# Cross attention on one core: the attention's cast and low part issued a slot later, and GpSimd's low probabilities put ahead of its normalization

## The chip, the cores and the metric

The kernel runs on one core of a Trainium2 chip. A core has a matrix engine (TensorE, in the profile PE, with its weight loads as PEld), a vector engine (VectorE, DVE), an engine for functions of one value (ScalarE, ACT), a general one (GpSimd, POOL) and one that here only issues transfers (SyncE, SP). Each works through its own queue of instructions in order, and semaphores tell one engine that another is done. The metric is the device time of the whole program in microseconds, as the median of several runs. Lower is better.

## The reference

For each of 32 sequences, 512 queries of 640 channels attend to 77 keys of a context in 20 heads of 32 channels. The context has 77 rows, so the object, others and image parts of the reference are empty, and what is left is this:

```python
q = _heads(hidden_states @ to_q_w)
s = jnp.einsum('bhqd,bhkd->bhqk', q, _heads(ehs_txt @ to_k_w)) / np.sqrt(HD)
p = jax.nn.softmax(s, axis=-1)
h_txt = jnp.einsum('bhqk,bhkd->bhqd', p, _heads(ehs_txt @ to_v_w))
out = _merge(h_txt) @ to_out_w + to_out_b
out = out + residual
```

Inputs and outputs are float32: x is (32, 512, 640), the context (32, 77, 1024), the output (32, 512, 640).

## The kernel before

**Two parts for each number.** [...] So each factor is held as a high part, its cast, and a low part, the original minus the cast. A product is three matmuls (`PAIRS`): high by high, high by low, low by high. The usual maker of such a pair is `split` (lines 102 to 104): ScalarE casts, then VectorE subtracts, so that the subtraction waits for the cast.

**The order is written out by hand.** After `manual_schedule` each engine runs its instructions in the order in which the program issues them. A first stage, some 272 us long, projects keys and values of all sequences and stores them in DRAM. Then comes the main loop: `slot(n)` for n = 0 to 159, where n = 5 b + j stands for batch (sequence) b and chunk j of four heads. `end()` finishes what hangs over.

**One slot.** In each slot several chunks are in work at different stages:

- `scores(n, t)` for t = 0 to 3 multiplies queries by keys on TensorE (L453) into the tile `sc` (three buffers), and VectorE takes the negated maximum of each head (L461, `nm`). `exps(n, t)` on ScalarE makes the exponentials into `pn` and their sums (L471).
- `queries(n + 1, ...)` makes the next chunk's queries (L434, tile `pq`), and `split_q(n + 1)` splits them (`qt`).
- For the chunk before, `sums(n - 1)` takes the reciprocals of the sums on VectorE (L481, `rs`), `normalize(n - 1, rs)` multiplies `pn` by them on GpSimd (L486), and `transpose_p(n - 1)` transposes them on VectorE into `z` (L493) and sends them to DRAM (L500).
- Two slots later `load_p` brings the transposed probabilities back (`raw`, L509 and L510). In slot n the chunk `taken` = n - 3 (`LAG`) is split: `cast_p` casts the first 128 rows of each half (L517, ScalarE), `rest_p` casts the last 64 (L523, ScalarE) and makes the low part of the first 128 on VectorE (L524), and `last_p` makes the low part of the last 64 on GpSimd (L531). All of it goes into the tile `pp`, of which there is one buffer.
- `values(taken)` multiplies these probabilities by the values: six matmuls into `pa` (L545), of which the last two read what `last_p` wrote. `sum_a` copies half of `pa` on ScalarE (L556) and adds it to the other on VectorE (L558, twice) into `aw`, of which there is one buffer. `split_a` splits this attention into `at` (L103 on ScalarE, L104 on VectorE; eight buffers).
- `piece(...)` is the output projection of an earlier batch: matmuls of `at` by the output weights into `po` (L584; two banks). `finish` adds each closed bank to the residual on VectorE (L613), which frees the bank. The first pieces of a batch read the `at` of chunk n - 4 in the slots j = 2 and j = 3.
- Beside these, `split_x` casts parts of the next input on ScalarE (L262) and subtracts on GpSimd (L263) in the slots j = 2 (two) and j = 3 (three), `transpose_x` transposes it on VectorE (L255), and `add_bias` adds the bias to the residual on GpSimd (L577).

**The order around the change.** At a slot's end ScalarE issues `exps(n, 3)` and then the cast of `at`, VectorE the two sums of `aw` and then the low part of `at`. The next slot begins with `cast_p` on ScalarE and the first maximum on VectorE, then `rest_p` on both, `sums` on VectorE. On GpSimd, `normalize` goes ahead of `last_p` in slots in which an output projection runs (`has_out`); in the first few slots it is the other way round. `take(m)`, used by the last slot and by `end()`, calls `values`, `sum_a` and `split_a` at once.

## Time and profile before

| | |
|---|---|
| median of 3 runs | 2055.46 us (2054.43 to 2056.07) |
| the profiled execution, its own time | 2056.36 us |
| its span, first to last instruction | 2054.2 us |
| mean granted TensorE clock | 0.991 |
| from the first `scores` to the last chunk's | 272 to 1999 us |
| a batch of five slots, in the steady part | 54.30 us |
| DMA, share of 16 engines in 330 to 1990 us | 0.84 |

How such a profile is read: the page lists for each engine its busy time with the share of the span and the number of instructions. Its groups show a line of the code, the engine, the operation, the tiles it writes and reads, the shape and the count; then the busy time in us, the mean time of one in ns, and the idle time of the engine just before them, with what ended most of it. The table of waits has who waited for whom, in total us, times and the longest. A timeline lists instructions of one engine or all in order: start in us, how long, engine, line, operation; like ones in a row are merged (x4), and idle time ahead of one stands in square brackets with what ended it. That releaser is inferred from semaphores: of several it names the last.

An instruction on VectorE or ScalarE can start some 0.1 us before the one ahead of it is shown to end.

### The profile page before, as it was taken

What the parts mean: (1) busy time and instruction counts of PE and PEld (TensorE: products, weight loads), DVE (VectorE), ACT (ScalarE), POOL (GpSimd) and SP (SyncE); (2) the same over time, 40 slices, a digit from 0 to 9 for tenths busy, and PEclk for the clock granted to TensorE, in tenths of its full rate; (3) what the DMA queues carried; (4) which work ended last, traced back from release to release, by engine and by line L of the source; (5) the groups of instructions that cost most, each with busy time, mean ns of one, the idle gap of its engine ahead of it and who ended that gap; (6) DMA issues with size and microseconds to landing.
All of it is one profiled execution on the core that took longest, in us unless ns stands there. A gap on an engine that the chain in (4) does not pass through costs nothing.

```text
span 2054.2 us, 36186 instructions
## 1 busy us (share of the span) xinstructions
PE 1952.5 (95%) x10332; PEld 1694.3 (82%) x10332; DVE 1464.6 (71%) x2334; ACT 1547.1 (75%) x6210; POOL 1002.7 (49%) x648
## 2 busy tenths in 40 slices
PE   9999997999999999999999999999999999999997
PEld 7787886888888888888888888888888888888886
DVE  4444447777777777777777777777777777777774
ACT  3232248888888888888888888888888888888882
POOL 1000125555555555555555555555555555555543
PEclk9999998999999999999999999999999999999998
DMA  9878778888888888888888888888888888888874
GB/s 185 200 182 232 183 199 210 228 215 218 217 213 211 223 212 212 212 210 218 211 221 214 218 212 220 218 213 214 219 215 209 223 215 213 212 213 214 214 191 137
DMA packets 568277, 431.26 MB, mean 210 GB/s; under 512 B 195344, under 2 KB 477072, under 8 KB 568080
## 3 DMA queue, kind: packets, MB, share of 16 engines
q1 hardware_dynamic: 564848, 417.65, 80.6%
q0 software_dynamic: 3136, 11.14, 1.5%
q8 instruction: 84, 1.38, 0.3%
q14 instruction: 113, 0.93, 0.1%
q10 hardware_dynamic: 96, 0.16, 0.0%
HBM read 247.17 MB, written 181.64 MB: 209 GB/s over the span
## 4 chain that ended last, share of the span: by engine, by line
PE 36%; DVE 15%; issue 15%; DMA 12%; POOL 10%; ACT 6%; SPq 5%; POOLq 0%; ACTq 0%; DVEq 0%
PE po L584 11%; PE pq L434 9%; PE pa L545 6%; POOL pn L486 6%; PE sc L453 5%; DMA pd<-z 5%; DVE pp L524 4%; POOL pp L531 4%; DMA raw<-pd 3%; DVE aw L558 3%; SPq L500 2%; DVE z L493 2%; PE pk L191 2%; DVE nm L461 2%; ACT at L103 2%
## 5 line engine op out<-in xcount | busy, mean ns | idle before, releaser
L471 ACT ACTIVATE pn<-sc,nm 128x77 f32<-128x77 f32 x2560 | 800.3, 332 | 48.6 <-DVE nm L461 33.7
L486 POOL TENSOR_TENSOR pn<-pn,rs 128x1232 f32<-128x1232 f32 x160 | 364.0, 2275 | 736.0 <-DVE rs L481 442.5
L584 PE MATMUL po<-wo_s,at 128*128 128x320 f32 x3840 | 629.3, 312 | 11.1 <-DVE xr L613 3.4
L434 PE MATMUL pq<-xt,wq_s 128*128 128x512 f32 x2400 | 606.0, 393 | 0.0
L584 PEld LDWEIGHTS po<-wo_s,at 128*128 128x128 f32 x3840 | 577.1, 189 | 28.1 <-DVE xr L613 22.7
L471 ACT ACTIVATION_READ_ACCUMULATOR pn<-sc,nm 128x1 f32 x2560 | 541.3, 211 | 0.0
L434 PEld LDWEIGHTS pq<-xt,wq_s 128*128 128x128 f32 x2400 | 437.0, 188 | 75.2
L453 PE MATMUL sc<-kb,qt 128*128 128x308 f32 x1920 | 378.5, 306 | 11.2 <-ACT pn L471 5.6
L461 DVE TENSOR_REDUCE nm<-sc 128x4 f32<-128x308 f32 x640 | 291.2, 456 | 132.3 <-PE sc L453 132.2
L453 PEld LDWEIGHTS sc<-kb,qt 128*128 128x128 f32 x1920 | 325.6, 189 | 55.2 <-ACT pn L471 10.9
L545 PE MATMUL pa<-pp,vb 128*128 128x512 f32 x960 | 291.0, 415 | 66.0 <-POOL pp L531 55.8
L493 DVE STREAM_TRANSPOSE z<-pn 128x1280 f32<-128x1280 f32 x160 | 241.8, 1511 | 116.1 <-POOL pn L486 94.6
L556 ACT COPY aw<-pa 64x1024 f32<-64x1024 f32 x160 | 162.0, 1012 | 165.0 <-PE pa L545 164.9
L545 PEld LDWEIGHTS pa<-pp,vb 128*128 128x128 f32 x960 | 164.4, 190 | 146.0 <-POOL pp L531 127.8
L104 DVE TENSOR_TENSOR at<-aw,at 128x512 fp32r<-128x512 f32 x160 | 138.7, 867 | 135.3 <-ACT at L103 135.3
L531 POOL TENSOR_TENSOR pp<-raw,pp 64x512 fp32r<-64x512 f32 x160 | 208.7, 1305 | 51.5 <-ACT pp L523 39.5
L558 DVE TENSOR_TENSOR aw<-pa,aw 64x512 f32<-64x512 f32 x320 | 216.0, 675 | 23.8 <-ACT aw L556 21.6
L263 POOL TENSOR_TENSOR xt<-xs,xt 128x512 fp32r<-128x512 f32 x160 | 203.3, 1296 | 34.8 <-ACT xt L262 34.7
L577 POOL TENSOR_TENSOR xr<-xr,bias 128x640 f32<-128x640 f32 x128 | 200.6, 1569 | 9.7
L524 DVE TENSOR_TENSOR pp<-raw,pp 128x1024 fp32r<-128x1024 f32 x160 | 194.3, 1215 | 6.5 <-ACT pp L517 6.5
L517 ACT CAST pp<-raw 128x1024 fp32r<-128x1024 f32 x160 | 168.7, 1055 | 3.7 <-DMA raw<-pd 3.7
L103 ACT CAST at<-aw 128x512 fp32r<-128x512 f32 x160 | 99.8, 624 | 71.8 <-DVE aw L558 71.5
(42 smaller groups left out, 1402.6 us busy)
## 6 DMA issues: line engine op xcount, KB each, us to landing
pd<-z SPq DMA_DIRECT2D x640, 160.0 KB, 3.3
raw<-pd SPq DMA_DIRECT2D x160, 512.0 KB, 4.0
xs<-in_x_dram SPq DMA_DIRECT2D x128, 320.0 KB, 5.8
xr<-in_x_dram SPq DMA_DIRECT2D x128, 320.0 KB, 3.6
out_dram<-xr SPq DMA_DIRECT2D x127, 320.0 KB, 3.6
raw<-pd SPq DMA_DIRECT2D x160, 128.0 KB, 4.2
v_dram<-vs SPq DMA_DIRECT2D x80, 192.0 KB, 3.9
k_dram<-ks POOLq DMA_DIRECT2D x20, 512.0 KB, 3.4
```

The source lines that it names most:

```text
L263: low.tensor_tensor(parts[1], src, parts[0].bitcast(F32), ALU.subtract)
L434: nc.tensor.matmul(pqs[n], wq_s[:, k, a, j * P : (j + 1) * P], xts[b, k][:, c, :], start=(k == 0 and m == 0), stop=(k == NC_ - 1 and m == 2),)
L453: nc.tensor.matmul(sc[:, :KCOLS], qt[:, a, t * P : (t + 1) * P], kb[:, j - GROUPS[g][0], c], start=(m == 0), stop=(m == 2),)
L461: nc.vector.tensor_reduce(nm, sc[:, :KCOLS].rearrange("p (h k) -> p h k", k=NKEY), AX.X, ALU.max, negate=True)
L471: nc.scalar.activation(pnb[n % 2][:, at, :NKEY], sc[:, i * NKEY : (i + 1) * NKEY], AF.Exp, bias=nm[:, i : i + 1], accum_out=sms[n][:, at : ...
L486: nc.gpsimd.tensor_tensor(pf, pf, rs.unsqueeze(2).to_broadcast([P, NQ * HPC, NKEY]), ALU.mult)
L493: nc.vector.transpose(z.rearrange("p b t j -> p t b j"), pn.rearrange("p (t h) k -> p t (h k)", t=NQ).rearrange("p t (b i) -> p t b i", i=Q),)
L524: nc.vector.tensor_tensor(pp[:, 2:4, :], raw[:, 0:2, :], pp[:, 0:2, :].bitcast(F32), ALU.subtract)
L531: nc.gpsimd.tensor_tensor(pp[64:, 4, :], raw[:64, 2, :], pp[:64, 4, :].bitcast(F32), ALU.subtract)
L545: nc.tensor.matmul(pas[n][:, p, :], vb[:, p, t, :], pp[:, c, :], start=(c == p), stop=(t == 1),)
L558: nc.vector.tensor_tensor(aw[64 * p : 64 * p + 64, 0], pa[:64, p], aw[:64, p], ALU.add)
L584: nc.tensor.matmul(pos[b, t, h][:, :HALF], ats[b * NC_ + j][:, a, t * P : (t + 1) * P], wos[0][:, j, c, h * HALF : (h + 1) * HALF], start= ...
```

## The change

`split_a` becomes two functions, the cast and the low part. Both are no longer called at the end of the slot that made `aw`, but in the next one: the cast on ScalarE behind `cast_p` and ahead of `rest_p`'s cast, the subtraction on VectorE behind `rest_p`'s and the reciprocals. On GpSimd `last_p` now goes ahead of `normalize` in every slot. `take` calls both halves one after the other, as before. The instructions and their number stay the same.

```diff
-    def split_a(n):
+    def high_a(n):
         if n >= N - NC_ + 1:
             at = xpool[0].tile([P, 2, S], FPR, tag="xt", name="at", bufs=7)
         else:
             at = late[0].tile([P, 2, S], FPR, tag="at", name="at", bufs=8)
-        aw = aws.pop(n)
-        split(at[:, 0, :], at[:, 1, :], aw[:, 0])
+        nc.scalar.copy(at[:, 0, :], aws[n][:, 0])
         ats[n] = at
+
+    def low_a(n):
+        at = ats[n]
+        nc.vector.tensor_tensor(
+            at[:, 1, :], aws.pop(n)[:, 0], at[:, 0, :].bitcast(F32), ALU.subtract
+        )
...
     def take(m):
         values(m)
         sum_a(m)
-        split_a(m)
+        high_a(m)
+        low_a(m)
...
         if taken is not None:
             cast_p(taken)
+        if n - 1 in takes:
+            high_a(takes[n - 1])
         s = scores(n, 0)
         if taken is not None:
             rest_p(taken)
         rs = sums(n - 1) if n else None
-        if taken is not None and not has_out:
+        if taken is not None:
             last_p(taken)
         if n:
             normalize(n - 1, rs)
-        if taken is not None and has_out:
-            last_p(taken)
+        if n - 1 in takes:
+            low_a(takes[n - 1])
         exps(n, 0, *s)
...
         exps(n, 3, *s)
-        if taken is not None:
-            split_a(taken)
```

## The prediction

> **What bounds the kernel now.** I read the page first, then the table of waits, then the timelines of single engines through one batch (1087.74 to 1142.03 us of the profiled execution). A "slot" is one turn of `slot(n)`; I date it from the first matmul of `scores(n, 0)`. Slots repeat exactly by j = n % 5, and a batch of five takes 54.30 us: 10.69, 10.66, 11.07, 11.61 and 10.26 for j = 0 to 4.

> ```profile
> PE 1952.5 (95%) x10332; PEld 1694.3 (82%) x10332; DVE 1464.6 (71%) x2334; ACT 1547.1 (75%) x6210; POOL 1002.7 (49%) x648
> L104 DVE TENSOR_TENSOR at<-aw,at 128x512 fp32r<-128x512 f32 x160 | 138.7, 867 | 135.3 <-ACT at L103 135.3
> ```

> TensorE is busy 95%, so the question is where the rest goes. The table of waits (who waits for whom: us in total, times, longest) says it:

> ```profile
> DVE at L104 <- ACT at L103: 135.3, 160, 1.0
> PEld pa L545 <- POOL pp L531: 127.8, 153, 3.4
> PE pa L545 <- POOL pp L531: 55.8, 82, 2.9
> PEld po L584 <- DVE xr L613: 22.7, 62, 3.6
> ```

> The matmuls of `values` wait for the last low probabilities (L531), and some of `piece` for an output bank that L613 empties. VectorE's 135.3 us before the low part of `at` are idle time in order of program. The timelines of TensorE, GpSimd and VectorE through the slot j = 3 that begins at 1120.16 (start us, us, instruction):

> ```profile
> 1125.78 1.09 PE L545 MATMUL pa<-pp,vb 128*128 128x512 f32 x4
> 1127.86 0.73 PE L545 MATMUL pa<-pp,vb 128*128 128x512 f32 x2 [0.98 <-DMA raw<-pd]
> ...
> 1129.03 2.90 PE L584 MATMUL po<-wo_s,at 128*128 128x320 f32 x18
> ```
> ```profile
> 1124.18 2.27 POOL L486 TENSOR_TENSOR pn<-pn,rs 128x1232 f32<-128x1232 f32 x1 [2.68 <-DVE rs L481]
> 1126.54 1.27 POOL L531 TENSOR_TENSOR pp<-raw,pp 64x512 fp32r<-64x512 f32 x1
> ...
> 1129.40 3.79 POOL L263 TENSOR_TENSOR xt<-xs,xt 128x512 fp32r<-128x512 f32 x3
> ```
> ```profile
> 1122.66 1.22 DVE L524 TENSOR_TENSOR pp<-raw,pp 128x1024 fp32r<-128x1024 f32 x1
> 1123.79 0.25 DVE L481 RECIPROCAL rs<-sm 128x16 f32<-128x16 f32 x1
> ...
> 1126.49 1.51 DVE L493 STREAM_TRANSPOSE z<-pn 128x1280 f32<-128x1280 f32 x1 [0.92 <-POOL pn L486]
> 1127.93 0.65 DVE L104 TENSOR_TENSOR qt<-pq,qt 128x512 fp32r<-128x512 f32 x1
> 1128.50 0.87 DVE L613 TENSOR_TENSOR xr<-po,xr 128x320 f32<-128x320 f32 x2
> ...
> 1132.11 1.63 DVE L104 TENSOR_TENSOR at<-aw,at 128x512 fp32r<-128x512 f32 x1 [1.01 <-ACT at L103]
> ```

> Two chains are to be seen. First, rs, normalization, L531, last two `pa`: the fifth `pa` starts 2.08 after the first where four steps of 0.23 make 0.92, so TensorE loses 1.16, and 0.11 at the sixth. Second, normalization, z, qt, the first xr (ends 1128.97), `po`: 18 matmuls start at 1129.03, which is 0.29 late. Read alike, the stall at `pa` is 0.27, 0.62, 0.98, 1.27 and 0.20 for j = 0 to 4, together 3.34; at `po` it is 0.37 (j = 0) and 0.29 (j = 3). Without all of it a batch would take 50.30, some 10.06 a slot.

> **The change, part by part.** Nothing is added or removed: the same casts, subtractions and products run. Three things move. I count from E, the end of `exps(n-1, 3)` on ScalarE; in the trace it lies at -0.29 to 0.87 after the slot's beginning.

> *The cast of `at` behind the probabilities'.* Now ScalarE runs at, L517, L523 one behind the other (starts 0.53 and 0.96 apart: 1121.00, 1121.51, 1122.46), and waits up to 1.07 for aw before it. Afterwards L517 starts at E and ends at E+1.05, the cast of `at` runs E+0.96 to 1.57, L523 E+1.49 to 2.10. The sum is the same; what goes is the wait for aw, which the long L517 covers, and where aw comes later than E+0.92 the cast waits for it again.

> *Its low part behind rs on VectorE.* L524 no longer stands behind it: E+1.12 to 2.34, rs to E+2.50. The low part (0.69) could then start at E+2.42; behind it in VectorE's queue is the maximum of `scores(n, 1)`, and for that waits `exps(n, 1)`.

> *GpSimd: L531 before normalization.* L523 ends E+2.10, and GpSimd starts some 0.15 after what it waits for (rs ends 1124.04, L486 starts 1124.18): E+2.25, 1.28 long, so it ends about E+3.55. TensorE's fifth `pa` wants it at 6.5 (j = 3) or 7.4 of an unstalled slot, 1.9 later even for E = 1.12: the whole 3.34 at `pa` is off TensorE's path. Normalization would follow at E+3.6; in the slot shown it started at E+3.15, in the five slots at E+3.85 in the mean.

> *What the low part meets.* At E+2.42 to 3.55 GpSimd is in L531, then in L486. A VectorE subtraction with both inputs in SBUF does not run beside GpSimd here: the `at` row above took 1.63 instead of 0.69 and ended at 1133.74, 0.55 behind the GpSimd `xt` that ended at 1133.19; this is so in all 30 such meetings of the steady part, and that is the 867 ns mean of the page. The reverse too: L531 beside L524 in the early slots took 1.74 (ended 1.13 behind L524). What happens between two GpSimd instructions back to back shows once (VectorE, then GpSimd):

> ```profile
> 274.44 0.83 DVE L104 TENSOR_TENSOR vs<-vs 128x416 fp32r<-128x416 f32 x1 [1.15 <-ACT vs L103]
> ```
> ```profile
> 273.53 2.89 POOL L263 TENSOR_TENSOR xt<-xs,xt 128x512 fp32r<-128x512 f32 x2 [3.61 <-ACT xt L262]
> ```

> VectorE's 0.59 became 0.83, and the GpSimd pair took 2.89, not 2.55: the waiting subtraction went between the two, and the second ended 1.15 behind it. So I take: low part ends E+3.55+0.55 = 4.10; normalization ends 2.28-0.14 later, E+6.24; the maximum runs E+4.02 to 4.45 and `exps(n, 1)` starts at E+4.5, where L517-to-exps spacing alone would give E+3.3. The bounds of this unseen price: no meeting at all (low part 0.69, normalization ends E+5.9), or VectorE served only behind both (E+6.46).

> [...]

> **Slot by slot.** Later steps by their spacing in the trace: z starts 0.03 behind normalization, the next maximum (nm3) 2.03 behind it, the first xr of j = 3 ends 2.52 behind it (1126.45 to 1128.97); nm3 waits for its scores too, 8.5 of an unstalled slot.
> - j = 4, E = -0.25: L524 waits for the first maximum (1.1), L531 ends 3.38, normalization 6.07, nm3 8.5, `exps(n, 3)` 9.17 to 10.42; period 10.06, next E 0.36.
> - j = 0, E = 0.36: normalization 6.60, nm3 8.66, xr 9.54; `po` needs it and the slot ends 1.05 later (9.64 and 10.69 now): 10.59 instead of 10.06. Next E -0.16.
> - j = 1: aw is ready at 0.96, L531 ends 3.62, normalization 6.31; nm3 8.48 by its scores: 10.04, next E 0.36.
> - j = 2: aw only at 1.33 (an xs transposition stands before it), L524 to 2.86, L531 3.99, low part 4.54, `exps(n, 1)` 4.92, `exps(n, 2)` 6.61, xt, aw, xt on ScalarE, `exps(n, 3)` 9.95 to 11.20: 10.08, next E 1.12 (0.87 now).
> - j = 3, E = 1.12: L531 ends 4.60, low part 5.15, normalization 7.29, first xr 9.80 (8.82 now). `po` starts 9.85 and the slot ends 2.74 later: 12.59, a loss of 0.98. The stall at `pa` turns up again at `po`.

> The first `po` of j = 3 reads this low part at 5.04 and waits 0.1; the later stall swallows it. In the queue of SP nothing moves: z ends at most 1 us later than now, and its DMAs feed loads two slots on.

> Sum: 10.59+10.04+10.08+12.59+10.06 = 53.36, a gain of 0.94 a batch. Some 30 batches' worth of slots run so; the head (272 us) and `end()`, which calls both halves together as before, stay. 30 x 0.94 = 28: the profiled span 2054.2 becomes 2026. The median of the runs, 2055.46, lies 1.3 above that span: 2027.

> **The rivals.**
> 1. *No meeting*: low part at E+2.42, `exps(n, 1)` E+3.5, normalization E+5.9. Then j = 0 takes 10.42, and with E = 0.88 j = 3 12.09; sum 52.69, 48 us gained, 2007. Against it are the 30 rows of 1.63. Chance 0.15.
> 2. [...] Chance 0.10.
> 3. *Normalization later than E+6.24* (slower): periods of j = 0 and 3 follow it one for one, so 0.47 more in each eats the 0.94. A place for it: L531 and L486 each resumed late behind VectorE's L524 and low part. At 0.7 more the batch is 54.76: 14 us more, 2069. Chance 0.13.
> 4. *Low part ahead of L531* at L524's end: normalization ends E+6.6, j = 0 10.95, j = 3 12.8, sum 53.9, 2043. Against it: L531 stands ready first. Chance 0.05, faster all the same.

> **How the numbers follow.** The forecast has 0.57, its own range 2010 to 2048 (0.6 a batch to either side, the error of some ten steps read to 0.05). Of it 0.49 is faster by over 0.2% (4 us, about what a measurement of this kernel tells from none), 0.04 within and 0.04 slower; with rivals 1 and 4 faster makes 0.69. Rival 3 reaches from within (0.02) to slower (0.11), rival 2 adds 0.10: same 0.06, slower 0.25. The range reaches down to rival 1 with some room (1995) and up to rival 3 (2069), leaving out rival 2.

> **What would show it.** In the profile after: `pa` waiting for L531 near nothing; the new low part of `at` at about 1.7 us in nearly every slot, not in one of five; L486 at 2.3 behind it or with its wait inside (2.7 to 2.9); `po` of j = 3 waiting some 2 us for xr L613; `exps` waiting for the maximum by 1 us a slot. [...] The forecast is wrong if j = 3 exceeds 13.5 or if `pa` still waits.

## The result, and the profile after

| kernel | median, us | ratio to before | batch (mean) | j = 0, 1, 2, 3, 4 |
|---|---|---|---|---|
| before | 2055.77 | 1 | 54.33 | 10.69, 10.68, 11.07, 11.62, 10.26 |
| changed | 2065.98 | 1.0046 (1.0033 to 1.0059) | 54.59 | 10.46, 10.08, 10.11, 13.86, 10.09 |

The last two columns are means over the batches of slots 10 to 154, read from the starts of the first `scores` matmuls in the profiled execution. Four of five slots became shorter, by 2.0 us together. The slot j = 3 became 2.24 longer and more than ate that.

The table of waits of the changed kernel has no line of weight in which `pa` waits for L531. What is new (L618 is the former L613, L589 the former L584):

```profile
ACT pn L471 <- DVE nm L461: 217.4, 182, 1.8
PEld po L589 <- DVE xr L618: 85.1, 63, 3.6
PE po L589 <- DVE xr L618: 65.3, 33, 3.4
```

The timelines of TensorE, GpSimd and VectorE in the slot j = 3 that begins at 1123.89 (start us, us, instruction) answer to those shown of before:

```profile
1130.03 1.56 PE L545 MATMUL pa<-pp,vb 128*128 128x512 f32 x6
1131.42 0.58 PE L453 MATMUL sc<-kb,qt 128*128 128x308 f32 x3
1133.99 4.45 PE L589 MATMUL po<-wo_s,at 128*128 128x320 f32 x18 [1.99 <-DVE xr L618]
```
```profile
1127.45 1.29 POOL L531 TENSOR_TENSOR pp<-raw,pp 64x512 fp32r<-64x512 f32 x1 [2.09 <-ACT pp L523]
1128.82 2.60 POOL L486 TENSOR_TENSOR pn<-pn,rs 128x1232 f32<-128x1232 f32 x1
```
```profile
1126.32 1.22 DVE L524 TENSOR_TENSOR pp<-raw,pp 128x1024 fp32r<-128x1024 f32 x1 [0.92 <-ACT pp L517]
1127.46 0.25 DVE L481 RECIPROCAL rs<-sm 128x16 f32<-128x16 f32 x1
1127.62 1.66 DVE L571 TENSOR_TENSOR at<-aw,at 128x512 fp32r<-128x512 f32 x1
...
1131.45 1.51 DVE L493 STREAM_TRANSPOSE z<-pn 128x1280 f32<-128x1280 f32 x1 [1.40 <-POOL pn L486]
1132.89 0.65 DVE L104 TENSOR_TENSOR qt<-pq,qt 128x512 fp32r<-128x512 f32 x1
1133.46 0.87 DVE L618 TENSOR_TENSOR xr<-po,xr 128x320 f32<-128x320 f32 x2
```

The six `pa` run in one piece. The low part of `at` takes 1.66 beside GpSimd, normalization ends at 1131.42, the first xr at 1133.93, and `po` starts right behind it after 1.99 of idling. Up to here it is the chain that was forecast. Then look at the length of the 18 `po`: 4.45, where the kernel before took 2.90 for the same 18. Three stretches (busy time and number of instructions for each engine, then the granted TensorE clock):

```profile
core 0: us, PE busy (x) PEld busy (x) DVE busy (x) ACT busy (x) POOL busy (x), PEclk, DMA share, GB/s
1131.80:1134.00 2.20, 0.21 (x3) 0.01 (x1) 2.20 (x4) 2.17 (x10) 1.78 (x2) 1.00 0.75 191
1134.00:1138.28 4.28, 4.28 (x19) 4.28 (x19) 2.09 (x4) 4.25 (x13) 3.09 (x3) 0.60 0.91 211
1146.00:1150.00 4.00, 4.00 (x26) 3.74 (x25) 2.96 (x7) 3.54 (x11) 0.00 (x0) 1.00 0.83 174
```

Behind the stall the granted clock is 0.60 in the mean: by the trace's clock records it is 0.5 from 1134.40 for 3.413 us. The matmuls then start 0.27 apart instead of 0.146. Of the 30 slots j = 3 from n = 8 to n = 153, 18 took 14.3 to 14.4 and two 13.9, each with a fall of the clock behind its stall; nine took 12.84, with none. The first, n = 8, took 14.37 without a fall: there TensorE also waits 0.57 for `qt` and 0.94 for the low part of `at`. The mean clock of the whole execution fell from 0.991 to 0.975.

### The profile page after: what moved, and what is told of

It is laid out like the page before. It is cut to its first block, busy times and chain, and to the rows that moved or that the text cites. A ratio compares the mean times of both kernels' runs of the same rounds, so it can differ in the third digit from the quotient of the medians.

```text
span 2065.0 us, 36489 instructions
## 1 busy us (share of the span) xinstructions
PE 1956.2 (95%) x10332; PEld 1737.1 (84%) x10332; DVE 1581.4 (77%) x2334; ACT 1540.4 (75%) x6210; POOL 1057.4 (51%) x648
## 4 chain that ended last, share of the span: by engine, by line
PE 40%; ACT 16%; issue 15%; DVE 13%; POOL 11%; DMA 3%; SPq 1%; POOLq 0%; DVEq 0%; ACTq 0%
PE po L589 15%; PE pq L434 11%; POOL pn L486 8%; ACT pn L471 6%; PE sc L453 5%; PE pa L545 5%; ACT aw L556 3%; POOL pp L531 3%; PE pv L191 2%; PE pk L191 2%; DVE at L571 2%; DVE aw L558 2%; DMA pd<-z 2%; DVE qt L104 2%; ACT pp L523 2%
## 5 line engine op out<-in xcount | busy, mean ns | idle before, releaser
L589 PE MATMUL po<-wo_s,at 128*128 128x320 f32 x3840 | 667.5, 323 | 81.6 <-DVE xr L618 65.3
L589 PEld LDWEIGHTS po<-wo_s,at 128*128 128x128 f32 x3840 | 606.8, 198 | 106.7 <-DVE xr L618 85.1
L531 POOL TENSOR_TENSOR pp<-raw,pp 64x512 fp32r<-64x512 f32 x160 | 217.5, 1360 | 662.4 <-ACT pp L523 589.4
L486 POOL TENSOR_TENSOR pn<-pn,rs 128x1232 f32<-128x1232 f32 x160 | 412.8, 2580 | 59.7 <-DVE rs L481 48.9
L461 DVE TENSOR_REDUCE nm<-sc 128x4 f32<-128x308 f32 x640 | 296.0, 467 | 111.8 <-PE sc L453 107.3
L493 DVE STREAM_TRANSPOSE z<-pn 128x1280 f32<-128x1280 f32 x160 | 241.8, 1511 | 115.6 <-POOL pn L486 100.4
L545 PE MATMUL pa<-pp,vb 128*128 128x512 f32 x960 | 253.3, 399 | 1.6 <-DVE pp L524 0.8
L524 DVE TENSOR_TENSOR pp<-raw,pp 128x1024 fp32r<-128x1024 f32 x160 | 208.1, 1301 | 45.6 <-ACT pp L517 44.4
L571 DVE TENSOR_TENSOR at<-aw,at 128x512 fp32r<-128x512 f32 x160 | 236.0, 1475 | 3.0 <-ACT at L566 3.0
L263 POOL TENSOR_TENSOR xt<-xs,xt 128x512 fp32r<-128x512 f32 x160 | 203.2, 1290 | 65.1 <-ACT xt L262 34.7
L545 PEld LDWEIGHTS pa<-pp,vb 128*128 128x128 f32 x960 | 175.3, 189 | 32.2 <-DVE pp L524 1.1
L517 ACT CAST pp<-raw 128x1024 fp32r<-128x1024 f32 x160 | 168.9, 1055 | 4.4 <-DMA raw<-pd 4.4
L191 PE MATMUL pk<-ct,wk_s 128*128 128x512 f32 (+1 forms) x600 | 139.3, 392 | 8.4 <-ACT ct L103 5.9
```

Of the source, the lines that this page charges most:

```text
L461: nc.vector.tensor_reduce(nm, sc[:, :KCOLS].rearrange("p (h k) -> p h k", k=NKEY), AX.X, ALU.max, negate=True)
L486: nc.gpsimd.tensor_tensor(pf, pf, rs.unsqueeze(2).to_broadcast([P, NQ * HPC, NKEY]), ALU.mult)
L493: nc.vector.transpose(z.rearrange("p b t j -> p t b j"), pn.rearrange("p (t h) k -> p t (h k)", t=NQ).rearrange("p t (b i) -> p t b i", i=Q),)
L531: nc.gpsimd.tensor_tensor(pp[64:, 4, :], raw[:64, 2, :], pp[:64, 4, :].bitcast(F32), ALU.subtract)
L545: nc.tensor.matmul(pas[n][:, p, :], vb[:, p, t, :], pp[:, c, :], start=(c == p), stop=(t == 1),)
L571: nc.vector.tensor_tensor(at[:, 1, :], aws.pop(n)[:, 0], at[:, 0, :].bitcast(F32), ALU.subtract)
```

## The experiments

Theory after the result: normalization comes later in j = 3, and through z and qt that delays the xr on which `po` waits. The stall is long enough to make the clock fall. The rivals were that the meeting of the low part with GpSimd is the loss by itself, and that the `po` were slow for a reason of their own.

| kernel | median, us | ratio to before |
|---|---|---|
| moved only | 1985.38 | 0.9649 (0.9633 to 0.9665) |
| GpSimd's order only | 2169.15 | 1.0539 (1.0518 to 1.0559) |
| change, xr first in j = 3 | 2017.66 | 0.9807 (0.9792 to 0.9822) |
| change, eight matmuls in the stall | 2037.60 | 0.9903 (0.9888 to 0.9918) |
| change, two matmuls in the stall | 2038.06 | 0.9905 (0.9890 to 0.9920) |
| change, low part with one SBUF input | 2010.17 | 0.9767 (0.9751 to 0.9783) |
| moved, xr first in j = 3 | 1976.64 | 0.9607 (0.9592 to 0.9621) |
| moved, xr first, GpSimd's new order in j = 3 | 1990.47 | 0.9680 (0.9657 to 0.9704) |

### Each half of the change alone

The move of `at` with GpSimd's old order:

```diff
-        if taken is not None:
+        if taken is not None and not has_out:
             last_p(taken)
         if n:
             normalize(n - 1, rs)
+        if taken is not None and has_out:
+            last_p(taken)
         if n - 1 in takes:
             low_a(takes[n - 1])
```

> The cast and the low part of at in the next slot as in the change, but GpSimd's old order (normalization, then L531). Theory (what costs is normalization's lateness: through z and qt it delays the first xr of j = 3, TensorE stalls there for 2.15 us, and in two of three batches the clock then falls to half for 3.4 us): the low part now starts before GpSimd is busy, 0.7 us long; normalization ends 0.9 earlier, at 5.25 behind the end of exps(n-1, 3); pa waits some 1.0 us in j = 3 only, po 0.3; no half-clock stretches; j = 3 about 11.5, a batch 52.1, time about 1990 (1980 to 2010). Rival (the meeting of VectorE's low part with GpSimd is the loss, whatever GpSimd's order): the low part still takes 1.6 us and the time stays above 2050.

It is 3.5% faster than before, as the theory had it, and a batch takes 51.98. In the timelines of its slot j = 3 from 1089.44 (GpSimd, VectorE, TensorE):

```profile
1092.91 2.53 POOL L486 TENSOR_TENSOR pn<-pn,rs 128x1232 f32<-128x1232 f32 x1 [2.21 <-DVE rs L481]
1095.51 1.28 POOL L531 TENSOR_TENSOR pp<-raw,pp 64x512 fp32r<-64x512 f32 x1
```
```profile
1092.68 0.63 DVE L571 TENSOR_TENSOR at<-aw,at 128x512 fp32r<-128x512 f32 x1
...
1097.48 0.87 DVE L618 TENSOR_TENSOR xr<-po,xr 128x320 f32<-128x320 f32 x2
```
```profile
1095.06 1.09 PE L545 MATMUL pa<-pp,vb 128*128 128x512 f32 x4
1096.84 0.74 PE L545 MATMUL pa<-pp,vb 128*128 128x512 f32 x2 [0.70 <-POOL pp L531]
1097.42 0.58 PE L453 MATMUL sc<-kb,qt 128*128 128x308 f32 x3
1098.01 2.91 PE L589 MATMUL po<-wo_s,at 128*128 128x320 f32 x18
```

The low part now starts 0.23 ahead of normalization and takes 0.63. Normalization waits inside its own row (2.53 for 2.28). `pa` stalls only in j = 3, and `po` follows the xr at once: 11.31 instead of 13.86.

GpSimd's new order with `at` cast and subtracted at the slot's end, as before:

```diff
-        if taken is not None and not has_out:
+        if taken is not None:
             last_p(taken)
         if n:
             normalize(n - 1, rs)
-        if taken is not None and has_out:
-            last_p(taken)
```

> Only GpSimd's order changed (L531, then normalization, in every slot); at is cast and subtracted at the slot's end as before. Theory (normalization's lateness): L524 still stands behind the low part of at, holds L531 up, and normalization ends later than in the kernel before by about 0.9; pa waits for nothing, but po of j = 3 waits 2 us and more for the first xr and the clock falls in many batches: 2060 to 2085. Rival (the meeting of the moved low part with GpSimd is the loss): without it the time falls below that of before, to some 2010.

The direction came as the theory had it and the rival's did not, but the size was missed by 84 us: 5.4% slower, j = 3 16.39. GpSimd and TensorE in the slot j = 3 from 1168.46:

```profile
1173.18 1.79 POOL L531 TENSOR_TENSOR pp<-raw,pp 64x512 fp32r<-64x512 f32 x1 [2.11 <-issue]
1175.05 2.27 POOL L486 TENSOR_TENSOR pn<-pn,rs 128x1232 f32<-128x1232 f32 x1
```
```profile
1176.08 0.58 PE L453 MATMUL sc<-kb,qt 128*128 128x308 f32 x3
1179.89 5.17 PE L584 MATMUL po<-wo_s,at 128*128 128x320 f32 x18 [3.23 <-DVE xr L613]
```

L531 takes 1.79 beside L524, normalization ends 8.86 into the slot (7.52 in the full change), the stall is 3.23, and in all 30 such slots the clock is at half behind it. The size was missed because normalization ends 2.6 later in j = 3 than in the kernel before, not 0.9, and because the half clock lasts two stretches, 6.83 us, in 28 of the 30. The low part of `at` takes 0.69 in all 160 slots here. So it need not meet GpSimd for the loss to arise: GpSimd's order alone makes it. The two halves are not additive: alone 72 us less and 112 more than the kernel before in the same comparison (2057.42), together 10 more.

### Is it the clock?

Eight matmuls that nothing reads, put ahead of the 18 `po` of j = 3:

```diff
+        if has_out and j == 3:
+            spare = ps.tile([P, S], F32, tag="sc", name="fill", bufs=3)
+            for _ in range(8):
+                nc.tensor.matmul(
+                    spare, wq_s[:, 0, 0, :P], wq_s[:, 0:4, 0, :P], start=True, stop=True
+                )
         if has_out:
             piece(bo_, first + 1)
```

> The change, with eight matmuls of 512 columns (1.8 us at full clock) into a spare bank ahead of the 18 po of j = 3: they are work that nothing reads, in the time that TensorE otherwise stalls. Theory (the stall makes the clock fall to half): TensorE is idle for under 0.5 us there, the clock stays whole, j = 3 takes 12.84 in every batch instead of in one of three, a batch 53.55, time 2030 to 2038. Rival (the 0.27 us a matmul have another cause): j = 3 stays at 14.38 in two of three batches and the time at 2066, or more by the added work.

```profile
1120.04 0.59 PE L453 MATMUL sc<-kb,qt 128*128 128x308 f32 x3
1120.46 2.00 PE L761 MATMUL fill<-wq_s 128*128 128x512 f32 x8
1122.60 2.90 PE L589 MATMUL po<-wo_s,at 128*128 128x320 f32 x18
```

TensorE's timeline shows that `po` starts no earlier in its slot (10.11), yet its 18 take 2.90 again; the granted clock is 1.00 from 318 to 1996 us (0.994 in the mean of the execution, 0.975 in the change). TensorE does more work, and the kernel is 28 us faster than the change. It is the clock, and the clock follows the stall.

How much idling is too much? In the change's steady part I cut the time at the clock records into stretches of 3.413 us (all falls lie on one such grid, within a few ns). In the 20 stretches ahead of a fall TensorE idled 1.96 to 1.99; the most idle stretches without a fall have 1.87 and 1.85. This also tells why a third of the slots escape, though their stall is as long (1.97 of idling in the slot from 1179.01): the grid runs on its own, and where it cuts the stall in two, neither part is long enough. A test of that with two matmuls only (`range(2)`):

> The change with two matmuls of 512 columns (0.46 us) instead of eight ahead of the 18 po of j = 3. In the runs so far the clock falls where TensorE was idle for 1.96 us or more of a stretch of 3.41 us, and never where it was idle for 1.87 or less. Theory (the idle share of a stretch decides): the stall's idle time falls from 2.0 to some 1.6, no clock falls in the steady part; j = 3 12.84 in every batch, time 2030 to 2040. Rival (any stall of this kind can make it fall, and eight matmuls filled it up): j = 3 is still 14.38 in a good part of the batches, time 2045 to 2066.

```profile
1066.48 2.91 PE L589 MATMUL po<-wo_s,at 128*128 128x320 f32 x18 [1.51 <-DVE xr L618]
```

2038.06: the stall still has 1.5 in one piece, no stretch has more than 1.52 of idle time, and the granted clock is 1.00 from 337 to 1992 us. One slot j = 3 of 30 was still above 14, the first (n = 8), in which the clock did not fall either. So in this stall the idle time within one stretch decides. The "never" of the expectation holds for the steady part alone: in the change itself, behind the last `scores` (2012.41 us), the clock falls at 2042.34 us after a stretch with 1.62 of idle time. The figures 1.87 and 1.96 are therefore no threshold for every pattern of work; what else counts is not shown here.

### What the meeting costs

The low part made from `aw` and the bank of `pa`, so that one input is in PSUM:

```diff
-            at[:, 1, :], aws.pop(n)[:, 0], at[:, 0, :].bitcast(F32), ALU.subtract
+            at[:, 1, :], aws.pop(n)[:, 0], held.pop(n)[:, 0, :], ALU.subtract
```

> The change, with the low part of at made from aw and the bank of pa instead of aw and its cast: the same length of work in the same place with one input in SBUF instead of two; the low part of at is not the reference's. Theory (the meeting with GpSimd costs as the prediction put it): the low part takes some 0.65 instead of 1.63, exps(n, 1) starts 1.0 earlier, normalization 0.3 earlier; j = 0 10.42, j = 3 12.1 with a stall of some 1.4 at po, under what makes the clock fall; a batch 52.7, time 2008 (1998 to 2018). Rival (the meeting costs nothing on the path): j = 3 stays at 12.84 or 14.38, time 2030 to 2066.

The low part made so is not `aw` minus its cast, so this kernel serves for the time alone. Measured 2010.17, with j = 0 10.43, j = 3 12.02 and a batch of 52.71. The view of the low part's line, of the change and of this kernel (count: ns least/median/most, first and last start, form):

```profile
L571 DVE TENSOR_TENSOR at<-aw,at x160: 621/1619/1673, 322.3 to 2054.4; 128x512 fp32r<-128x512 f32 x160
```
```profile
L573 DVE TENSOR_TENSOR at<-aw,pa x160: 623/627/690, 322.3 to 1995.0; 128x512 fp32r<-128x512 f32 x160
```

In the same place, beside L531, 1.62 becomes 0.63. Against the kernel with the stall filled that is 27 us. So two parts of about one size are lost in the change: some 28 us by the clock, some 27 by the meeting. Without both, TensorE still idles 1.68 ahead of `po`, not the 1.4 expected, and the clock does not fall (1.00 from 340 to 1967 us). Against the move alone (1985.38) another 25 us are left, most of them in j = 3 (12.02 for 11.31), where normalization ends 0.7 later: they go with GpSimd's order itself, though no run takes them apart further.

### The xr ahead of z

In j = 3, `piece(bo_, first)` and `finish()` are issued before `transpose_p`, on top of the change:

```diff
+        early = ahead and has_out and j == 3
+        if early:
+            piece(bo_, first)
+            finish()
         if n and has_out:
             transpose_p(n - 1)
...
-            piece(bo_, first)
+            if not early:
+                piece(bo_, first)
...
-        if j == 3:
+        if j == 3 and not early:
             finish()
```

> The change, and in j = 3 the two xr of the banks closed there are issued ahead of z on VectorE instead of behind qt. Theory: the first xr no longer waits for normalization; the stall at po in j = 3 (2.15 us and 0.11 per matmul behind it) goes, and with it the half-clock stretches; ScalarE's chain then sets the slots j = 2 and 3; a batch of 52 to 52.5, time 1985 to 2010. Rival (the 18 po of j = 3 run at 0.27 us for a reason of their own, not for the stall before them): they stay at 0.27 in two of three batches, time 2025 to 2040.

The stall and the falls of the clock in j = 3 went, as the theory had it (10.70 in the mean). The time, 2017.66, missed the expectation by 8 us, because j = 0 grew to 12.09. TensorE in that slot, from 1071.42:

```profile
1079.93 1.03 PE L589 MATMUL po<-wo_s,at 128*128 128x320 f32 x6
1082.52 1.15 PE L589 MATMUL po<-wo_s,at 128*128 128x320 f32 x6 [1.55 <-DVE xr L618]
```

Here `exps(n - 1, 3)` ends 1.99 into the slot instead of 0.35. ScalarE, held up some 1.2 a slot by the maximum behind the low part, could catch up in the long j = 3 of the change; j = 3 is now short, and the stall moves to the next bank that waits for an xr behind z. On the kernel with `at` moved only, ScalarE is not held up:

> The kernel with the cast and low part moved and GpSimd's old order (1985 us), and in j = 3 the two xr ahead of z. Theory: with ScalarE not held up, the 0.27 at po in j = 3 goes and nothing is handed on to j = 0; the 0.98 at pa in j = 3 stays, since L531 still comes behind normalization: j = 3 11.05, a batch 51.7, time 1977 (1970 to 1984). Rival: z, now 0.7 later behind the two xr, delays qt and nm so that nothing is gained: 1985 or more.

1976.64, j = 3 11.03, a batch 51.73: as expected, and the fastest kernel of this study, 3.9% under before. Its `pa` still waits in j = 3. With the same edit, GpSimd's new order was then used in j = 3 alone:

```diff
+        low_first = not has_out or j == 3
-        if taken is not None and not has_out:
+        if taken is not None and low_first:
             last_p(taken)
```

> As the kernel with the two xr ahead of z and GpSimd's old order, but in j = 3 alone L531 goes ahead of normalization. Theory: the 0.98 at pa in j = 3 goes; the low part meets GpSimd in this slot alone, and its lag is taken up in j = 4: j = 3 about 10.3, a batch 51.1 (50.8 to 51.5), time 1957 (1948 to 1970). Rival (the lag is handed on through ScalarE to j = 0, as with the two xr ahead of z in the full change): j = 0 over 11, time 1975 or more.

1990.47, where 1957 was expected: slower again. j = 3 is 10.11, but j = 4 is 11.37, and the stall at `pa` stands there, in TensorE's timeline of the slot from 1101.32:

```profile
1107.83 1.09 PE L545 MATMUL pa<-pp,vb 128*128 128x512 f32 x4
1109.95 0.73 PE L545 MATMUL pa<-pp,vb 128*128 128x512 f32 x2 [1.03 <-POOL pp L531]
```

`exps(n - 1, 3)` ends 2.1 into this slot, where it ends 0.15 into it without the new order. The lag is handed on, as the rival had it, though to j = 4 and not to j = 0.

## Why the prediction was wrong

The forecast was 2027 and faster; the kernel is 10 us slower, at 2066. Point by point:

- *The stall at `pa` goes.* Right in every slot.
- *The low part meets GpSimd, about 1.7, and goes between L531 and normalization.* Right: median 1.62, over 1.2 in 134 of 160; normalization 2.60 with its wait inside. Normalization ends E+6.16 in j = 0 (E = 0.35), forecast E+6.24. The first rival (no meeting, 2007) is the kernel with one SBUF input: 2010.
- *`exps(n, 1)` waits about 1 us for the maximum.* Right: 217 us in 182 waits, 1.2 each.
- *j = 0, 1, 2, 4 at 10.59, 10.04, 10.08, 10.06.* Measured 10.46, 10.08, 10.11, 10.09.
- *Sign and rivals.* Normalization was not later than forecast from E (the third rival). No run shows what the second had at a chance of 0.10, a low part served only behind both GpSimd instructions (E+6.46): it took 1.62 in the median and 1.67 at most. Both slower cases named a wrong cause. The slower case that came was in none of them; that the third rival's 2069 lies near the measured 2066 is chance.
- *j = 3: "`po` starts 9.85 and the slot ends 2.74 later: 12.59".* This is the step that failed. The start was mis-sized a little: 10.10, because `exps(n - 1, 3)` ended at 1.37 and not at 1.12; the nine undisturbed slots took 12.84, 0.25 more, which is some 7 us in 30 batches. The 2.74 behind it is what failed: it was read from a slot that ran at full clock, and a stall was taken as a mere delay of what follows. The sum has no term for the clock and gives no reason for leaving it out. In 20 of 30 slots the stall took the clock down, and 2.74 became 3.8 to 4.3: 18 times 1.5 and twice 1.0 make some 29 us. Without it the change would have come out at some 2037, as both kernels with matmuls in the stall did, and the forecast's own range would have held. The prediction's own sign of being wrong, j = 3 above 13.5, came (13.86).

The trace of before could have warned: it had no stall of that length in its steady part (the most idle stretches of the grid have 1.5, but for one of 2.67 at 352 to 356 us, behind which its clock record shows 0.5 for 3.413 us too). The prediction put the loss in j = 3 at 0.98 and wrote that the stall at `pa` "turns up again at `po`", without asking how long TensorE would then stand in one piece.

## What to carry to other kernels

Two short stalls of TensorE in a slot may be cheaper than one long one: before stalls are gathered into one, look at how long TensorE idles in one piece, and count the time behind it at half the clock if it is long enough (here 1.96 us of idling within one stretch of 3.413 us, and a clock of 0.5 for the next 3.413 us). When a change has two halves, run each alone: here one half was worth 3.5% and the other took it back. Before GpSimd's order is changed, look for what stands behind its later result on VectorE, and for VectorE subtractions with two SBUF inputs beside it: that of `at` took 1.63 beside GpSimd in 30 slots of the kernel before and 0.69 in the other 130, and 0.63 with one input in PSUM in the kernel made for it.
